# Transformer block in fp32: order of the first loads, engine of two normalized tiles, queue of the last store

## The chip, the core and the metric

The kernel runs on one core of one Trainium2 chip. The metric is device time in microseconds: 620.65 is the median of three runs (619.79 to 624.14). The engines are named as the profile names them: PE is TensorE's matmul and PEld its weight load, DVE is VectorE, ACT ScalarE, POOL GpSimd, SP SyncE. A "q" behind a name (SPq, ACTq) is that engine's instruction queue, from which DMAs are issued.

## What is computed

The input x has 8 batches of 1024 rows with 256 channels, in fp32. Each row is normalized, and the normalized x feeds an attention without softmax and a feed-forward net; both results are added to x.

```python
x = L0_attn_x
xn = _layernorm(x, axis=-1)
x = x + _L0_attn_ref(xn, qkv_w, qkv_b, proj_w, proj_b) + _L0_ffn_ref(xn, W1, b1, W2, b2)

# attention: 16 heads of 16 channels
qkv = (x @ qkv_w + qkv_b).reshape(b, n, 3, H, D)
q, k = _l2norm(q), _l2norm(k)
kv  = einsum('bhnd,bhne->bhde', k, v)
out = einsum('bhnd,bhde->bhne', q, kv)  # then @ proj_w + proj_b

# feed-forward: 256 -> 1024 -> 256
relu(hidden_states @ W1 + b1) @ W2 + b2
```

## The kernel before

**Tiling.** One batch is 1024 rows, held as NT = 8 tiles of 128 rows (one row to a partition), in two halves of HT = 4 tiles. A partition's four rows of a half lie next to each other in memory, so that a load of two tiles reads 2 KB per partition. Most products are made by a scheme with seven block products in place of eight; its sums of blocks are made by POOL and DVE (`sums_of_a`, `sums_of_b`, L179 to L192, L223 to L235).

**Stages of a batch.** Normalize x (`norm_stats`, L239: mean and variance on DVE and the square root on ACT; `norm_scale`, L253: the reciprocal, on DVE; `norm_apply`, L262: xn itself). Turn xn so that channels lie on partitions. Project to q and k (`project`, L311, or `project_by_sums`, L387). Take the norms of q and k. Make the hidden layer (`hidden`, L628). Mix k and xn into a 256 by 256 matrix and fold it with the projection (`mix_g`, `mix_kv`, `mix_m`). Make the second layer together with the attention's product (`second`, L769), add x, and store. The loop over batches is at L935. While one batch is in its hidden and second layers, the next is projected and the one after that is normalized and turned.

**What sets the order.** The kernel is written under a manual schedule (L112): on each engine the instructions run in the order in which the Python code emits them, and every engine's queue is served in that order. DMAs go out on SP's queue, apart from two of the last stores. PSUM is used as banks from a pool of seven (L76, L92), and a new tile of the pool waits until the bank it gets is read out. The x of one batch is in a single buffer (`xs`, one buffer, L99), so the load of the next batch waits until the xn of all eight tiles has been made.

**The start, where two of the three edits are.** SP issues, in this order: tiles 0 and 1 of x (L126), the q and k columns of the weights (L127, L120), tiles 2 to 7 of x in three loads of two tiles (L128, L102), the bias of q and k (L129; `load_qkvb`, L123, spreads 512 numbers over 128 partitions, 256 KB), b1 (L131), w1 in two loads of 512 KB (L134), and the v columns of weights and bias (L135, L136). PE first turns the identity 16 times (L888 to L890). Tiles 0 and 1 are normalized on DVE one by one (L900 to L905), turned by PE and copied out of PSUM by ACT (`turn_tile`, L893 to L898). Tiles 2 and 3 follow as a pair, with xn on ACT (L906 to L908). POOL makes sums of w1 (L909, run at L184).

Then `project(0, ...)` (L931) runs over the eight tiles. For each tile t, PE makes a product of two halves (kc = 0 and 1, L328) and DVE adds the bias while it reads the product out of PSUM (L334). ACT squares the result (L338) and DVE sums the squares (L339); these are held back until tile 3. Between the two halves of tile 1 it emits `tiles_2_3` (L912): turn tiles 2 and 3, then the statistics of 4 and 5 and of 6 and 7, their scales, and their xn. Between the two halves of tile 3 it emits `tiles_4_to_7` (L922): turn tiles 4 to 7, turn b1 (L926), copy it (L927) and make the sums of x on POOL (L928, L929). So DVE's queue around there holds, in order: the bias add of tile 0, the statistics of tiles 4 to 7, their scales, two xn, the bias adds of tiles 1 and 2, the copy of b1, the bias add of tile 3.

The third argument of `norm_scale` says who makes xn:

```python
if on_act:      # one more DVE operation, -mean * rstd ("nmr"), L258
    nc.scalar.activation(xn, xt, AF.Identity, bias=nmr..., scale=rstd...)  # L269
else:
    nc.vector.tensor_scalar(xn, xt, mean, rstd, ALU.subtract, ALU.mult)    # L273
```

For tiles 4 and 5 ACT makes it, for tiles 6 and 7 DVE.

**The end, where the third edit is.** In the last batch the upper half of the result is turned back by PE (`back_on_pe`, L812), added to x by DVE (L822) and stored in three pieces (L867 to L884): tiles 0 and 1 of the half, then tile 2, both issued by ACT, then tile 3, issued by SP. SP issues the four stores of the other half just before (`store`, L808 to L810), and waits for all DMAs at the end.

Of the kernel before, what the change touches and what calls it, by code (L numbers as in the profile page):

```python
# [16 lines left out]
def kernel(  # L17
# [34 lines left out]
    nc = tc.nc  # L52
# [28 lines left out]
    def rows_v(v, b, n):  # L81

        return v[b].rearrange("(n p t) c -> n p t c", n=2, p=P)[n]

    def squares_v(v, b, n, j):


        return v[b].rearrange("(n s r t) (j c) -> n j s r t c", n=2, s=S, r=R, j=R)[n, j]

    def bank(shape, name):  # L90

        return psum.tile(shape, F32, tag="bank", name=name)  # L92
# [3 lines left out]
    def load(b, cuts=(0, HT, NT)):  # L96

        if b not in xs:
            xs[b] = one.tile([P, NT, C], F32, tag="x", name=f"x_{b}")  # L99
        for i, j in zip(cuts, cuts[1:]):  # L100
            n = i // HT
            nc.sync.dma_start(  # L102
                out=xs[b][:, i:j, :], in_=rows_v(x, b, n)[:, i - n * HT : j - n * HT, :]
            )
# [13 lines left out]
    def load_wqkv(cols):  # L118
        for k in range(KC):
            nc.sync.dma_start(out=wqkv_sb[:, k, cols], in_=qkv_w[ts(k, P), cols])  # L120

    def load_qkvb(cols):
        nc.sync.dma_start(out=qkvb_sb[:, cols], in_=qkv_b[cols].partition_broadcast(P))  # L123
# [1 line left out]
    of_qk, of_v = slice(0, 2 * C), slice(2 * C, 3 * C)  # L125
    load(0, (0, 1, 2))  # L126
    load_wqkv(of_qk)  # L127
    load(0, (2, 4, 6, 8))  # L128
    load_qkvb(of_qk)  # L129
    b1_rows = one.tile([FC, P], F32, tag="gT", name="b1_rows")  # L130
    nc.sync.dma_start(out=b1_rows, in_=b1.rearrange("(k p) -> k p", p=P))  # L131
    w1_sb = const.tile([P, KC, INTER], F32, tag="w1", name="w1_sb")
# [120 lines left out]
    def norm_scale(b, tiles, on_act):  # L253
        i, mv, rstd = stats[b, tiles[0]]
        nc.vector.reciprocal(rstd, rstd)
        if on_act:
            nmr = small.tile([P, NT], F32, tag="nmr", name=f"nmr_{b}_{i}")[:, : len(tiles)]
            nc.vector.scalar_tensor_tensor(nmr, mv[:, :, 0], -1.0, rstd, ALU.mult, ALU.mult)  # L258
            for t in tiles:
                stats[b, t] += (nmr,)  # L260
# [500 lines left out]
    def product(dst, lhs, rhs, start, stop):  # L761

        for n, (l, r) in enumerate(zip(lhs, rhs)):
            nc.tensor.matmul(  # L764
                dst, l, r, start=start and n == 0, stop=stop and n == len(lhs) - 1,
                skip_group_check=True,
            )

    def second(b, early=lambda: None, between=lambda: None):  # L769

        xq, hT, hS, qT, (M, Mt) = xqs[b], hTs[b], hSs[b], qTs[b], Ms[b]
        a11, a12, s3, a22 = (
            [hT[:, i + k * FH, ts(n, HP), :, :] for i in range(FH)] + [qT[:, k, ts(n, HP), :, :]]
            for n in range(2) for k in range(2)
        )
        s1, s2, s4 = ([hS[:, s, i] for i in range(FH + 1)] for s in range(3))
        b11, t3, b21, b22 = (
            [w2_sb[:, i + k * FH, ts(m, HC)] for i in range(FH)] + [M[:, k, ts(m, HC)]]
            for k in range(2) for m in range(2)
        )  # L780
        t1, t2, t4 = ([w2t[:, s, i, :] for i in range(FH)] + [Mt[:, s, :]] for s in range(3))

        def tmp(name):
            pool = work if name in ("u2", "yt") else one
            return pool.tile([P, HP, P, 2], F32, tag=name, name=f"{name}_o_{b}")

        def add(dst, p, q):
            nc.vector.tensor_tensor(dst, p, q, ALU.add)
            return dst

        def turn_back(n, m, y):

            yt = tmp("yt").rearrange("p a b c -> p (a b c)").rearrange(
                "p (u w r c) -> p u w r c", w=2, r=R, c=S
            )
            nc.vector.transpose(  # L796
                yt.rearrange("p u w r c -> p u r w c"),
                y.rearrange("p u (s r) w -> p u r w s", r=R),
            )
            xh = xq[:, n, :, :, ts(m, S)].rearrange("p r t c -> p t r c")  # L800
            nc.gpsimd.tensor_tensor(xh, xh, yt.rearrange("p u w r c -> p (u w) r c"), ALU.add)  # L801

        def join(n, m, bank_, u):
            y = tmp("y")
            nc.vector.scalar_tensor_tensor(y, bank_, ob[:, 2, m : m + 1], u, ALU.add, ALU.add)
            turn_back(n, m, y)

        def store(n):  # L808
            for j in range(R):
                nc.sync.dma_start(out=squares_v(out, b, n, j), in_=xq[ts(j, S), n])  # L810

        def back_on_pe(m, y, tiles, name):  # L812


            tp = bank([P, HT, R, S], f"tp{name}_{b}")
            for t in tiles:
                nc.tensor.transpose(
                    tp[:, t].rearrange("p j c -> p (j c)"), y[:, t // 2, :, t % 2], ident
                )
            xh = xs[b].rearrange("p (n t) (j m c) -> n m p t j c", n=2, m=2, c=S)[1, m]  # L820
            at = slice(tiles[0], tiles[-1] + 1)
            nc.vector.tensor_tensor(xh[:, at], xh[:, at], tp[:, at], ALU.add)  # L822

        a, c_, d, e = (bank([P, HP, P, 2], f"po{s}_{b}") for s in "acde")

        if b < B - 1:
            parts = [lambda r: r]
        else:
            parts = [lambda r: r[:, 0], lambda r: r[:, 1, :, 0], lambda r: r[:, 1, :, 1]]
        ds = [parts[0](d)] + [  # L830
            part(bank([P, HP, P, 2], f"po{s}_{b}")) for s, part in zip("fg", parts[1:])
        ]
        product(a, b11, a11, True, False)
        u1 = tmp("u1")
        nc.scalar.copy(u1, a)
        product(c_, t2, s2, True, True)
        u2 = add(tmp("u2"), c_, u1)
        early()
        u3 = tmp("u3")
        for du, part in zip(ds, parts):  # L840
            product(du, t3, [part(r) for r in s3], True, False)
            add(part(u3), du, part(u2))
        between()

        product(e, t1, s1, True, False)
        if b < B - 1:
            join(1, 1, e, u3)
        else:
            y22 = tmp("u1")
            nc.vector.scalar_tensor_tensor(y22, e, ob[:, 2, 1:2], u3, ALU.add, ALU.add)  # L850
        yield
        product(a, b21, a12, False, True)
        y = tmp("y")
        nc.scalar.activation(y, a, AF.Identity, bias=ob[:, 2, 0:1])  # L854
        turn_back(0, 0, y)
        product(e, b22, s4, False, True)
        join(0, 1, e, u2)
        store(0)
        if b < B - 1:
            product(d, t4, a22, False, True)  # L860
            join(1, 0, d, u2)
            store(1)
        else:
            back_on_pe(1, y22, range(HT), "o22")
            y21 = tmp("y")

            def last_store(eng, t, n):  # L867
                eng.dma_start(
                    out=rows_v(out, b, 1)[:, t : t + n, :], in_=xs[b][:, HT + t : HT + t + n, :]
                )  # L870

            for k in range(len(ds) + 1):
                if k < len(ds):
                    part = parts[k]
                    product(ds[k], t4, [part(r) for r in a22], False, True)
                    nc.vector.scalar_tensor_tensor(
                        part(y21), ds[k], ob[:, 2, 0:1], part(u2), ALU.add, ALU.add
                    )
                if k == 1:
                    back_on_pe(0, y21, (0, 1), "o21_0")  # L880
                    last_store(nc.scalar, 0, 2)
                elif k > 1:
                    back_on_pe(0, y21, (k,), f"o21_{k}")
                    last_store(nc.scalar if k == 2 else nc.sync, k, 1)  # L884
        yield


# [24 lines left out]
    def tiles_2_3():  # L912
        for t in (2, 3):
            turn_tile(t)
        norm_stats(0, (4, 5))
        norm_stats(0, (6, 7))
        norm_scale(0, (4, 5), True)
        norm_scale(0, (6, 7), False)
        norm_apply(0, (4, 5))
        norm_apply(0, (6, 7))  # L920

    def tiles_4_to_7():  # L922
# [6 lines left out]
        sums_of_x(0, 1)  # L929

    project(0, {1: tiles_2_3, 3: tiles_4_to_7}, 3, False)  # L931
    s3_of_x(0)
    load(1)
    load_rest()
    for b in range(B):  # L935
# [15 lines left out]
        if b + 1 < B:  # L951
# [4 lines left out]
            def early():  # L956
                if b + 2 < B:
                    norm_stats(b + 2, range(NT))
                    norm_scale(b + 2, range(NT), True)

            def between():
                g_sums(b + 1, 2)
                if b > 0:
                    norms_of_q(b + 1)
# [49 lines left out]
```

## Time and profile before

| what | before |
|---|---|
| median of three runs | 620.65 us (619.79 to 624.14) |
| the profiled execution: its own time | 622.37 us |
| its span | 620.6 us |
| PE busy | 611.1 us, 98% |
| POOL busy | 421.1 us, 68% |
| DVE busy | 411.6 us, 66% |
| ACT busy | 211.8 us, 34% |
| mean granted TensorE clock | 0.995 |
| DMA | 43.32 MB, mean 70 GB/s |

The span runs from the first to the last instruction of the profiled execution; its own time is the device time of that same execution. A line of the timeline shows the start, the length, the engine, the line of code, the operation, what is written and read, and how many instructions were merged. In square brackets stand the idle time before it and what ended it. A line of the chain of waits shows the start, the length and what the chain ran through. A line of the windows shows the stretch, its length, the busy time of PE, PEld, DVE, ACT and POOL, then the granted clock, the DMA engines' busy share and GB/s. A matmul of 128 by 128 with 512 columns in fp32 shows as two records, and some records can be missing.

### The profile page before, as it was taken

To read this page: it belongs to the slowest core of one execution; us is meant where nothing else is said; L and a number is where in the kernel's file an instruction comes from. 1 tells how busy PE (TensorE), PEld (TensorE's weight loads), DVE (VectorE), ACT (ScalarE), POOL (GpSimd) and SP (SyncE) were. 2 spreads that over 40 slices of the span, in tenths; PEclk is the share of its full clock that TensorE was granted. 3 is DMA by queue.
4 is the path that set the end of the run, shared out by engine and by line. 5 is a ranking of instruction groups with operands and counts; after the bars stand their busy time and mean duration, and the time that the engine had idled before them with its cause. 6 is when DMAs were issued, how large, how long until landed. Compare 5 with 4: busy or idle time off the path is not lost.

```text
span 620.6 us, 6646 instructions
## 1 busy us (share of the span) xinstructions
PE 611.1 (98%) x2027; PEld 346.5 (56%) x2027; DVE 411.6 (66%) x736; ACT 211.8 (34%) x361; POOL 421.1 (68%) x346
## 2 busy tenths in 40 slices
PE   8999999999999999999999999999999999999996
PEld 4465446447554566446564474644846557555454
DVE  5778654778647777587756876657865678528823
ACT  4445514252233522344142432415224352103500
POOL 2485997399925998179964799349992499914701
PEclk9899999999999999999999999999999999999999
DMA  6743100590016700285004830058101560004202
GB/s 212 152 69 70 67 1 21 116 191 13 0 45 135 159 2 0 65 156 121 0 1 100 186 54 1 10 127 179 26 0 33 121 118 1 0 5 99 68 1 68
DMA packets 139796, 43.32 MB, mean 70 GB/s; under 512 B 135912, under 2 KB 136816, under 8 KB 139760
## 3 DMA queue, kind: packets, MB, share of 16 engines
q1 hardware_dynamic: 139472, 42.50, 30.7%
q10 hardware_dynamic: 288, 0.39, 0.2%
q8 instruction: 16, 0.26, 0.2%
q14 instruction: 20, 0.16, 0.1%
HBM read 19.80 MB, written 8.39 MB: 45 GB/s over the span
## 4 chain that ended last, share of the span: by engine, by line
PE 95%; DVE 2%; DMA 1%; SPq 0%; issue 0%; ACT 0%; DVEq 0%; ACTq 0%
PE poa L764 11%; PE poe L764 11%; PE pod L764 10%; PE pha L640 8%; PE phe L640 8%; PE phd L640 8%; PE poc L764 6%; PE phc L640 4%; PE pq L328 4%; PE pqe L403 3%; PE pqa L403 3%; PE pqd L403 3%; PE gpe L570 2%; PE gpd L570 2%; PE gpa L570 2%; PE pqc L403 2%
## 5 line engine op out<-in xcount | busy, mean ns | idle before, releaser
L801 POOL TENSOR_TENSOR xq<-xq,yt_o 128x512 f32<-128x512 f32 x30 | 37.9, 1264 | 122.5 <-DVE yt_o L796 122.5
L647 ACT ACTIVATE hT<-hT,b_sb 128x512 f32<-128x512 f32 x96 | 68.9, 722 | 63.2 <-DVE hT L652 58.4
L188 POOL TENSOR_TENSOR hS<-hT 128x512 f32<-128x512 f32 x31 | 46.5, 1500 | 40.2 <-ACT hT L647 40.2
L640 PE MATMUL pha<-xnT,w_sb 128*128 128x512 f32 x128 | 65.4, 592 | 0.0
L764 PE MATMUL poa<-hT,w_sb 128*128 128x512 f32 x128 | 57.6, 592 | 0.0
L381 ACT ACTIVATE sq<-qk 128x512 f32<-128x512 f32 x48 | 28.9, 626 | 71.1 <-DVE qk L409 59.1
L652 DVE TENSOR_TENSOR hT<-phe,u 128x512 f32<-128x512 f32 x64 | 43.7, 684 | 6.7 <-PE phe L640 4.8
L190 POOL TENSOR_TENSOR hS<-hT,hS 128x512 f32<-128x512 f32 x31 | 39.6, 1277 | 2.4
L189 POOL TENSOR_TENSOR hS<-hS,hT 128x512 f32<-128x512 f32 x31 | 39.5, 1274 | 2.4
L796 DVE STREAM_TRANSPOSE yt_o<-y_o 128x512 f32<-128x512 f32 x30 | 33.0, 1100 | 11.4 <-ACT y_o L854 9.1
L192 POOL TENSOR_TENSOR hT<-hT 128x512 f32<-128x512 f32 x31 | 40.0, 1291 | 0.0
L764 PEld LDWEIGHTS poa<-hT,w_sb 128*128 128x128 f32 x128 | 23.8, 190 | 24.7 <-issue 24.2
L640 PEld LDWEIGHTS pha<-xnT,w_sb 128*128 128x128 f32 x128 | 23.8, 190 | 23.4 <-issue 22.5
L666 ACT COPY u<-pha 128x512 f32<-128x512 f32 x32 | 18.4, 575 | 51.6 <-PE pha L640 51.6
L652 DVE TENSOR_TENSOR u<-phc,u 128x512 f32<-128x512 f32 x32 | 21.8, 682 | 19.7 <-ACT u L666 10.6
L647 ACT ACTIVATE hT<-pha,b_sb 128x512 f32<-128x512 f32 x32 | 21.8, 683 | 33.2 <-PE pha L640 33.2
L640 PE MATMUL phe<-xS,w1t 128*128 128x512 f32 x64 | 32.7, 592 | 0.0
L640 PE MATMUL phd<-xnT,w_sb 128*128 128x512 f32 x64 | 32.7, 592 | 0.0
L640 PE MATMUL phc<-xS,w1t 128*128 128x512 f32 x64 | 32.7, 592 | 0.0
L640 PE MATMUL phd<-xnT,w1t 128*128 128x512 f32 x64 | 32.7, 592 | 0.0
L640 PE MATMUL phe<-xS,w_sb 128*128 128x512 f32 x64 | 32.7, 592 | 0.0
L269 ACT ACTIVATE xn<-x,nmr,rstd 128x256 f32<-128x256 f32 x56 | 28.5, 587 | 7.0 <-PE gpd L570 4.1
(200 smaller groups left out, 1318.8 us busy)
## 6 DMA issues: line engine op xcount, KB each, us to landing
xq<-in_L_attn_x_dram SPq DMA_DIRECT2D x60, 128.0 KB, 3.6
out_dram<-xq SPq DMA_DIRECT2D x60, 128.0 KB, 2.9
x<-in_L_attn_x_dram SPq DMA_DIRECT2D x14, 512.0 KB, 4.5
xnT<-turn_x SPq DMA_DIRECT2D x112, 64.0 KB, 2.1
qT<-turn_q SPq DMA_DIRECT2D x112, 64.0 KB, 2.2
w_sb<-in_L_ffn_W_dram SPq DMA_DIRECT2D x2, 512.0 KB, 7.8
w_sb<-in_L_ffn_W_dram SPq DMA_DIRECT2D x8, 128.0 KB, 3.2
x<-in_L_attn_x_dram SPq DMA_DIRECT2D x3, 256.0 KB, 4.3
```

The lines of the kernel that those rows point to most:

```text
L188: eng.tensor_tensor(s1, a21, a22, ALU.add)
L189: eng.tensor_tensor(s2, s1, a11, ALU.subtract)
L190: eng.tensor_tensor(s4, a12, s2, ALU.subtract)
L192: eng.tensor_tensor(a21, a11, a21, ALU.subtract)
L403: nc.tensor.matmul(dst[:, w, :], a[:, g, :, w], rhs, start=start and w == 0, stop=stop, skip_group_check=True,)
L570: nc.tensor.matmul(dst, l[:, t, :], r[:, t, :], start=start and t == 0, stop=stop and t == HT - 1, skip_group_check=True,)
L640: nc.tensor.matmul(dst, lhsT, rhs, start=start, stop=stop, skip_group_check=True)
L647: nc.scalar.activation(block(i, n, m), src, AF.Relu, bias=b1_sb[:, fc : fc + 1])
L652: nc.vector.tensor_tensor(dst, p, q, ALU.add)
L764: nc.tensor.matmul(dst, l, r, start=start and n == 0, stop=stop and n == len(lhs) - 1, skip_group_check=True,)
L796: nc.vector.transpose(yt.rearrange("p u w r c -> p u r w c"), y.rearrange("p u (s r) w -> p u r w s", r=R),)
L801: nc.gpsimd.tensor_tensor(xh, xh, yt.rearrange("p u w r c -> p (u w) r c"), ALU.add)
```

## The change

There are three edits. The bias of q and k is issued after tiles 2 and 3 of x and ahead of tiles 4 to 7. The xn of tiles 6 and 7 of the first batch is made by ACT, with one more small DVE operation for their `nmr`. The last of the three stores of x is issued by ACT instead of SP.

```diff
     load(0, (0, 1, 2))
     load_wqkv(of_qk)
-    load(0, (2, 4, 6, 8))
+    load(0, (2, 4))
     load_qkvb(of_qk)
+    load(0, (4, 6, 8))
     b1_rows = one.tile([FC, P], F32, tag="gT", name="b1_rows")
...
-            def last_store(eng, t, n):
-                eng.dma_start(
+            def last_store(t, n):
+                nc.scalar.dma_start(
                     out=rows_v(out, b, 1)[:, t : t + n, :], in_=xs[b][:, HT + t : HT + t + n, :]
                 )
...
                 if k == 1:
                     back_on_pe(0, y21, (0, 1), "o21_0")
-                    last_store(nc.scalar, 0, 2)
+                    last_store(0, 2)
                 elif k > 1:
                     back_on_pe(0, y21, (k,), f"o21_{k}")
-                    last_store(nc.scalar if k == 2 else nc.sync, k, 1)
+                    last_store(k, 1)
...
         norm_scale(0, (4, 5), True)
-        norm_scale(0, (6, 7), False)
+        norm_scale(0, (6, 7), True)
         norm_apply(0, (4, 5))
         norm_apply(0, (6, 7))
```

## The prediction

> **What bounds it.** I read the page first (its span, granted clock, shares of the chain), then the chain of waits over the first 45 us, then the timeline of each engine around the long link found there, then windows for the clock, and last SP's queue at the end.
>
> ```profile
> span 620.6 us, 6646 instructions
> ...
> PEclk9899999999999999999999999999999999999999
> ...
> PE 95%; DVE 2%; DMA 1%; SPq 0%; issue 0%; ACT 0%; DVEq 0%; ACTq 0%
> ```
>
> TensorE sets the end for 95% of the span, so a microsecond counts only where PE waits, where its clock is low, or after its last matmul. The second digit of the clock row, an 8, is the one dip before the tail. The chain of waits shows what stands ahead of it (start, length, what):
>
> ```profile
> 4.02 6.95 DMA qkvb_sb<-in_L_attn_qkv_b_dram
> ...
> 11.06 0.69 DVE qk L334
> ...
> 14.11 2.32 DVE xn L273 x2
> 16.43 0.61 DVE qk L334
> ...
> 17.34 9.55 PE pq L328 x18
> ```
>
> The bias lands at 10.97; VectorE, whose queue is in order, holds the statistics of tiles 4 to 7 behind the add that needs it (L334), then two xn that take 2.32, then the next add. What PE, ScalarE and GpSimd did meanwhile, from the timelines:
>
> ```profile
> 9.91 3.60 PE L328 MATMUL pq<-wqkv_sb,xnT 128*128 128x512 f32 x8
> 14.42 1.28 PE L897 MATMUL tpx<-ident,xn 128*128 128x128 f32 x6 [0.91 <-ACT xn L269]
> 16.57 0.41 PE L897 MATMUL tpx<-ident,xn 128*128 128x128 f32 x2 [0.87 <-DVE xn L273]
> 17.08 0.26 PE L926 MATMUL b_ps<-ident,b_rows 8*128 8x8 f32 x1
> ...
> 13.78 1.08 ACT L269 ACTIVATE xn<-x,nmr,rstd 128x256 f32<-128x256 f32 x2
> ...
> 14.96 1.32 POOL L184 TENSOR_TENSOR w_sb<-w_sb 128x512 f32<-128x512 f32 x1
> ```
>
> PE ends the first half of tile 3's product at 13.51 and begins its second at 17.27: 3.76 us, of which 0.91 + 0.87 + 0.10 = **1.88 is waiting** and 1.88 (1.28 + 0.41 + 0.19) is transposes. The granted clock follows (window, length, busy of PE, PEld, DVE, ACT, POOL, then PEclk):
>
> ```profile
> 16.50:17.50 1.00, 0.83 (x4) 0.60 (x5) 1.00 (x2) 0.48 (x2) 1.00 (x1) 0.81 0.15 16
> 17.50:18.50 1.00, 1.00 (x2) 0.48 (x3) 0.20 (x2) 0.95 (x2) 1.00 (x2) 0.50 0.86 270
> ...
> 20.50:21.50 1.00, 1.00 (x3) 0.39 (x2) 0.90 (x3) 0.81 (x2) 0.98 (x1) 0.98 1.18 183
> ```
>
> 0.81 means half clock from 17.12, 0.98 full clock from 20.54: 3.42 us at 0.50 with PE busy throughout, so **1.71 us of work lost**.
>
> **The change, part by part.**
>
> (1) Bias ahead of x tiles 4 to 7. No transfer is added; on SP the bias is issued at 3.07 instead of 4.02, the two loads of x 0.48 later each, all behind them at the same place. Landings by the DMA view: x(2,4) issued 2.60 + 4.1 = 6.7; x(4,6) 3.07 + 4.3 = 7.4; x(6,8) 3.54 + 5.3 = 8.8; bias 4.02 + 6.9 = 10.9. So the steps between landings are 0.7, 1.4 and 2.1. If the queue drains in order, the bias follows x(2,4) by 0.7 to 2.1: 7.4 to 8.8, I take 8.0. By one shift of issue alone it would land at 3.07 + 6.9 = 10.0, my outer bound. The x loads follow; the same three transfers still lie ahead of the last landing, so x(6,8) comes by about 10.9; I take 10.5, and x(4,6) 9.3. Outer bound for x(6,8): 4.02 + 8.3, the longest landing of this stretch (w1), 12.3. Its old earliness was worthless: x(6,8) lay unused from 8.8 to 12.55.
>
> VectorE then: nmr of tiles 2 and 3 ends at 8.45 as now; add 0 until 9.15; statistics of tiles 4 and 5 (0.75 + 0.30) from 9.3; of 6 and 7 from 10.5 to 11.55; the reciprocals and two nmr (0.15 each, with ScalarE's 0.29 root of 6 and 7 between) 11.85 for the first nmr, 12.25 for the second. Now the first ends at 13.73. Adds 1 and 2 follow by 13.6, not 17.6.
>
> (2) xn of tiles 6 and 7 by ScalarE. VectorE loses two operations that took 2.32 together; the same form took 0.41 and 0.42 at 4.48 and 5.00, where GpSimd was idle. Here each ended just after one of GpSimd's L184 (13.73 + 1.27 = 15.00, 14.96 + 1.32 = 16.28). I count 2.32, since GpSimd's sums start when w1 lands, which the change doesn't move; if VectorE reached these before 12.38 they would cost 0.83. Added on VectorE: one nmr, 0.16. Added on ScalarE: two ACTIVATE at 0.54 (the pair took 1.08), **ahead of the four copies of tpx**, which now start only after xn of tile 7. ScalarE: xn from 11.95, four by 0.54, done 14.15; copies at 0.41 until 15.8. PE: transposes from 13.51 with xn of 4 and 5 ready (12.5, 13.05), of 6 ready at 13.6 for 14.3, of 7 at 14.15 for 14.7; transposes done by 15.15. The b1 transpose, which now waits for add 1 (0.34 of PEld), finds it done. So tile 3's second half starts at 13.51 + 1.88 = 15.39, and tile 4's product (needed at 16.25) finds its copy made at 14.6. Gain **1.88**. The slack is 0.55: if xn of tile 7 ends after 14.7, each microsecond is lost one for one. SP's load of the next x waits for the last xn (7.3 us of its queue's waits); it leaves at about 14.2 instead of 16.5, with the proj and w2 loads behind it. Its first reader is at 33.77, so this is worth nothing, and costs nothing.
>
> What is late next? GpSimd still ends its sums of x at 21.5; first need is phc, at about 24 after the move, so it hides. VectorE between 16.3 and 25.3 has five adds (0.69) and eight reductions (0.68), 8.9 us in 9, so it just follows; tile 7's product comes at 23.1 and the chain beyond it (adds, roots, L652 up to PE's 0.7 wait at 37.02) moves as a block. Nothing up to the end is tied to an absolute time.
>
> (3) The clock. The Trainium skill (TensorE: Matmul & The Clock Gate, Part 1, "What's actually happening") puts the half clock after at least one idle window of about 3.4 us. Here no wait exceeds 0.91 us and half of the stretch was transposes, yet the clock fell; the row decides: waits summing to half of such a stretch suffice. By the rule this dip isn't due to the waits and stays, gain 0; by the row it goes with them, gain **1.71**. I take the row, for the profiled execution.
>
> (4) The last store, of one tile, by ScalarE. Now it sits on SP behind the four stores of xq:
>
> ```profile
> 614.84 1.36 SPq L810 DMA_DIRECT2D out_dram<-xq  x1
> 616.29 1.04 SPq L868 DMA_DIRECT2D out_dram<-x  x1
> ```
>
> And the windows of that time, which end in DMA share and GB/s:
>
> ```profile
> 616.00:617.00 1.00, 0.00 (x0) 0.00 (x0) 0.00 (x0) 0.00 (x0) 0.00 (x0) 1.00 1.02 288
> 617.00:618.00 1.00, 0.00 (x0) 0.00 (x0) 0.00 (x0) 0.00 (x0) 0.00 (x0) 0.94 1.07 282
> ```
>
> The x it stores is ready at 615.76, and ScalarE's queue has been free since 615.56. From ScalarE it would leave at 615.85 and by the row's 3.4 land at 619.25 instead of 619.7; the xq store of 614.84 lands at 619.34, so 0.35 by this row. But DMA: Bandwidth & Descriptors (Issuing engines are not separate DMA queues) says that issuing from several engines saves only issue time, as all run on the same 16 engines; these are full from 616 to 618 and drain the same bytes, which gives 0. I take **0.2**.
>
> **Sum.** Span 620.6 - 1.88 - 1.71 - 0.2 = 616.8. The profiled execution took 622.37, 1.77 outside the span: 618.6. It lies 1.72 above the median of the runs shown, just what the dip costs, so I read the median as a run without it: 620.65 - 1.88 - 0.2 = 618.6 as well. Predicted 618.6, 0.3% less than now: inside the 1% (6.2 us) that a measurement of this kernel tells from no change.
>
> **Rivals.**
> - The likeliest, chance 0.53: as summed, 618.6; its own range is 617.6 to 619.5 by the 0.55 of slack, the ends of (4) and the scatter of the runs.
> - A part of the wait stays, 0.2: bias at 10.0, or x(6,8) at 12.1. First xn near 13.5, xn of tile 7 done at 15.7, second half of tile 3 at about 16.4: gain 0.9, with 0.2 of the tail 619.6. For it: the bias's 6.9 us to landing; against: three other landings before it came every 0.7 to 1.4.
> - The median run carries the dip too, 0.14: 620.65 - 1.88 - 1.71 - 0.2 = 616.9. For it: the one clock trace there is; against: the 1.72 between it and the median.
> - The gain is given back, 0.06: VectorE or a slow-clock stretch elsewhere takes it, 620.5. Against: the block argument above.
> - Slower, 0.07: **x(6,8) comes too late behind the bias.** From its landing to xn of tile 7 are 3.65 us (10.5 to 14.15); that ended at 16.43 before, so it decides from a landing at 12.8. At 13.8 PE starts 1.0 later than now: 620.65 + 1.0 - 0.2 = 621.5. It needs 9.8 us from issue, more than the 8.3 of the slowest here.
>
> **Chances and range.** 616.7 to 620.4 takes in the first three and half of the fourth's neighbourhood, leaving about 0.15 outside. Over 1% means under 614.4 or over 626.9; no case reaches either, so what I leave there is for a mechanism that I don't see: 0.02 faster, 0.03 slower, 0.95 within.
>
> **What would show it.** Right: the chain's bias link of 6.95 shorter and ending before 9, no VectorE xn from 14 on, ScalarE's four xn in one row from about 12, PE's waits of 0.91 and 0.87 gone, tile 3's second half at about 15.4, PEclk without the 8, last store from ACT near 615.8 less the shift. Wrong: statistics of 6 and 7 waiting on DMA beyond 11, PE waiting on ACT's xn, or a longer tail than 619.7 - 615.76 = 3.9 us from last add to last landing.

## The result, and the profile after

| | before | changed |
|---|---|---|
| median of 22 runs each | 620.67 us | 619.52 us |
| lowest to highest | 619.68 to 624.14 | 618.56 to 621.94 |
| ratio to before, 95% interval | | 0.9977 (0.9966 to 0.9988) |
| profiled execution, its span | 622.37, 620.6 | 619.26, 617.4 |

The change gains about 1.2 us, 0.2%: less than the 1% named ahead, but clear of zero. 618.6 was forecast, and 619.6 for the rival in which a part of the wait stays; the rival's number came out. The two profiled spans differ by 3.2 us, far more than the medians. Why, is the main lesson here.

The page of the changed kernel (lines of its code are one higher than before from L130 on):

```profile
span 617.4 us, 6649 instructions
...
PEclk9999999999999999999999999999999999999999
```

The 8 in the second slice of the clock row is gone. The chain of waits after:

```profile
2.59 4.59 DMA x<-in_L_attn_x_dram
...
8.93 0.61 ACT xn L270
9.58 0.45 PE tpx L898 x2
10.04 0.69 DVE qk L335
...
13.10 0.85 DVE nmr L259
13.97 1.10 ACT xn L270 x2
...
15.71 7.94 PE pq L329 x18
```

The chain now runs through the load of x tiles 2 and 3 (4.59) and names PE's transposes ahead of the add of 10.04. Those write another tile; what the add was waiting for is still the bias, which was issued at 3.06 and landed 6.9 later, at 9.94:

```profile
3.06 0.43 SPq L123 DMA_DIRECT2D qkvb_sb<-in_L_attn_qkv_b_dram x1
...
10.04 0.69 DVE L335 TENSOR_TENSOR qk<-pq,qkvb_sb 128x512 f32<-128x512 f32 x1 [1.14 <-PE tpx L898]
```

The view of the bias's tile gives the two loads that write it (6.9 is this one):

```profile
DMA to landing us min/median/max: 4.9/5.9/6.9
```

The add follows the landing by 0.1, as before (10.96 and 11.06). VectorE's two xn of 2.32 are gone. PE's timeline:

```profile
9.58 0.93 PE L898 MATMUL tpx<-ident,xn 128*128 128x128 f32 x4 [0.72 <-ACT xn L270]
10.35 3.60 PE L329 MATMUL pq<-wqkv_sb,xnT 128*128 128x512 f32 x8
13.79 0.60 PE L898 MATMUL tpx<-ident,xn 128*128 128x128 f32 x4
14.63 0.93 PE L898 MATMUL tpx<-ident,xn 128*128 128x128 f32 x4 [0.23 <-ACT xn L270]
15.49 0.22 PE L927 MATMUL b_ps<-ident,b_rows 8*128 8x8 f32 x1
```

The second half of tile 3's product starts at 15.64 (17.27 before). Of the waits 0.91 + 0.87, 0.23 is left, but one of 0.72 has come up ahead of tile 2: PE ends the first half of tile 3 at 13.95 instead of 13.51. The clock stays at full where it fell before (granted clock is the third number from the end):

```profile
16.00:17.00 1.00, 1.00 (x3) 0.39 (x2) 0.19 (x1) 1.00 (x3) 1.00 (x2) 1.00 0.86 238
17.00:18.00 1.00, 1.00 (x4) 0.49 (x3) 1.00 (x2) 0.20 (x1) 1.00 (x2) 1.00 1.02 377
```

The last add ends 3.23 earlier (612.53 against 615.76): 1.63 from the earlier start, and the other 1.6 I put down to the clock. The tail after it is 4.9 against 4.8.

**Two numbers by which the runs are read.** First, in all twelve profiles without a clock dip after it (the changed kernel and eleven of the experiments), the profiled execution's time less the start of tile 3's second half is 603.57 to 604.00. Apart from the queue of the last store, all that differs between these kernels is ahead of that start. In the two profiles with a dip after it (before and store only) the difference is 605.1 and 605.3, so there the dip cost 1.3 to 1.5. Second, each run has its mean granted clock: 0.997 or more in some, 0.996 or less in others, which are some 2 us longer. These are called runs with a dip. The sorting isn't perfect: the profiled run of bias order only has a dip and a mean of 0.997, and counts as one without. Three later groups of runs of the kernel before hold 56, 57 and 17 of them: with a dip 19, 24 and 9 (40% in all), median 622.3 to 622.5; without, 620.31, 620.55 and 620.64. The changed kernel has 1 of 22 with a dip, and 619.44 without. For the 22 runs of before beside it only times are on record.

### The profile page after: what moved, and what is told of

It is laid out like the page before. It is cut to its first block, busy times and chain, and to the rows that moved or that the text cites. A ratio compares the mean times of both kernels' runs of the same rounds, so it can differ in the third digit from the quotient of the medians.

```text
span 617.4 us, 6649 instructions
## 1 busy us (share of the span) xinstructions
PE 608.3 (99%) x2027; PEld 345.5 (56%) x2027; DVE 409.8 (66%) x735; ACT 212.3 (34%) x363; POOL 420.4 (68%) x346
## 4 chain that ended last, share of the span: by engine, by line
PE 95%; DVE 2%; DMA 1%; ACT 1%; issue 0%; SPq 0%; DVEq 0%; ACTq 0%
PE poa L765 11%; PE poe L765 11%; PE pod L765 10%; PE pha L641 8%; PE phe L641 8%; PE phd L641 8%; PE poc L765 6%; PE phc L641 4%; PE pq L329 4%; PE pqd L404 3%; PE pqa L404 3%; PE pqe L404 3%; PE gpe L571 2%; PE gpd L571 2%; PE gpa L571 2%; PE pqc L404 2%
```

## The experiments

| kernel | tile 3's second half, profile | median of runs without a dip | with a dip | ratio to before (95%) |
|---|---|---|---|---|
| changed | 15.64 | 619.44 | 1 of 22 | 0.9977 (0.9966 to 0.9988) |
| bias order only | 17.66 (dip ahead of it) | 619.63 | 2 of 22 | 0.9982 (0.9971 to 0.9992) |
| ACT's xn only | 16.36 | 620.12 | 5 of 14 | 0.9996 (0.9983 to 1.0010) |
| store only | 16.48 | 620.67 | 8 of 14 | 1.0007 (0.9994 to 1.0019) |
| bias and xn | 15.05 | 619.18 | 1 of 19 | 0.9971 (0.9960 to 0.9982) |
| waits filled | 17.09 | 620.88 | 0 of 22 | 0.9990 (0.9980 to 1.0000) |
| bias not spread | 15.58 | 619.00 | 0 of 10 | 0.9957 (0.9941 to 0.9973) |
| bias in the middle | 16.00 | 620.58 | 7 of 14 | 0.9997 (0.9982 to 1.0013) |
| bias spread by PE | 15.08 | 620.35 | 0 of 22 | 0.9979 (0.9966 to 0.9991) |
| stats first, ACT's xn | 14.54 | 618.16 | 0 of 6 | 0.9946 (0.9931 to 0.9961) |
| stats first | 14.30 | 617.98 | 0 of 6 | 0.9942 (0.9928 to 0.9957) |
| stats first, xn and store by ACT | 13.87 | 618.41 | 0 of 6 | 0.9954 (0.9935 to 0.9972) |
| bias spread by PE, later | 17.82 | 621.81 | 0 of 12 | 1.0002 (0.9989 to 1.0015) |

The first four experiments are compared with the group of 620.31 without a dip, the next four with that of 620.55, the last four with that of 620.64. The ratio is that of all runs, with and without a dip; so a part of it is the dips that a kernel lacks.

**Bias order only.** The kernel before with the first hunk of the change alone.

> Only the bias moves ahead of tiles 4 to 7 of x; xn of tiles 6 and 7 stays on DVE. Theory (each edit takes away a part of PE's wait, the two overlap): the bias lands near 10.0, the statistics of 6 and 7 end near 12.5 as in the changed kernel, DVE begins xn of 6 near 13.1 and is held by GpSimd's running L184 again (two xn take over 2 us), so tile 7 is turned near 15.5 and tile 3's second half begins near 16.1 instead of 17.27: 0.8 to 1.2 us faster. Rival one (the order of loads is all of it): 15.6, 1.2 to 1.6 faster, as the changed kernel. Rival two (order is worth nothing, because the x tiles come as much later as the bias comes earlier): 17.0 or more, within 0.3 of before.

Without a dip it gains 620.31 - 619.63 = 0.7, just below the theory's 0.8 to 1.2. Its profile shows the cost of the move at its worst:

```profile
10.64 1.05 PE L898 MATMUL tpx<-ident,xn 128*128 128x128 f32 x4 [1.84 <-ACT xn L270]
11.49 5.21 PE L329 MATMUL pq<-wqkv_sb,xnT 128*128 128x512 f32 x8
```

x(2,4), with the bias right behind it, landed 5.6 after issue instead of 4.1; PE waited 1.84 for tile 2, and the clock fell behind it (granted 0.83, 0.50 and 0.82 in the windows from 10 to 16); the eight records took 5.21 instead of 3.60. VectorE's two xn took 2.65 beside GpSimd's sums, as the theory had it.

**ACT's xn only.** The last hunk alone.

> Only xn of tiles 6 and 7 goes to ACT; the loads keep their order. Theory: the bias lands near 11.0 as before, ACT's four xn begin at 13.8 and end at 16.0, tile 3's second half begins near 16.7: 0.4 to 0.8 us faster. Rival one (order of loads is all): 17.2, within 0.2. Rival two (the held xn on DVE is all of it): 15.6 to 16.0, 1.2 or more faster. The sum of this run's gain and the bias-only run's gain against the gain of both tells whether they overlap.

0.2 without a dip, below the theory's 0.4 to 0.8, and the interval of its ratio takes in one. In its profile tile 3's second half comes 5.7 after the bias landed, against 6.3 in three profiles with xn on VectorE (see below): 0.6 in the theory's favour, which nine runs don't confirm. 0.7 + 0.2 stands against 1.1 for both (620.31 - 619.18): no overlap is seen, but sums this small don't rule one out.

**Store only.** `last_store(nc.scalar, k, 1)` in the kernel before.

> Only the last store of x is issued by ACT. Theory after the first traces: nothing, since the DMA engines drain the same bytes: last add to end of span stays at 4.84 to 4.87, time within 0.2 of before. Rival (the 0.2 to 0.35 of the prediction): that stretch 4.5 to 4.65, time 0.2 to 0.35 less.

Last add to end of span is 4.9. Over all profiles that stretch is 4.8 to 5.1 in the seven with SP's last store and 4.9 to 5.3 in the seven with ACT's: no gain. PE's timeline shows something else, which matters for the size of the whole change. The start of this kernel is that of before, but here the bias landed at 10.20, not 10.96, and the waits are smaller:

```profile
13.66 1.24 PE L897 MATMUL tpx<-ident,xn 128*128 128x128 f32 x6 [0.36 <-ACT xn L269]
15.77 0.41 PE L897 MATMUL tpx<-ident,xn 128*128 128x128 f32 x2 [0.87 <-DVE xn L273]
```

Tile 3's second half starts at 16.48, 6.3 after the bias, as in the profile of before (10.96 and 17.27).

**Bias and xn, without the store edit.**

> The changed kernel without its store edit. Theory: the same as the changed kernel, 1.1 to 1.6 us faster than before, tile 3's second half at 15.6, last add to end of span 4.84. Rival (the store edit gives 0.2 to 0.35): 0.2 to 0.35 us slower than the changed kernel.

Its median without a dip is 0.26 below the changed kernel's 619.44. With the store-only run (0.36 above before) that hints at a small loss by the store edit; neither is resolved.

**The waits filled.** Transposes of the identity, overwritten by the real ones:

```diff
+        for _ in range(fill):       # 4 for tiles 4 and 7, else 0
+            nc.tensor.transpose(tp[:, 0, :], ident, ident)
         for kc in range(KC):
             nc.tensor.transpose(tp[:, kc, :], xns[0][:, t, ts(kc, P)], ident)
```

> The kernel before, with four transposes of the identity ahead of tile 4's and four ahead of tile 7's (about 0.85 us each time, inside PE's waits of 0.91 and 0.87); their result is overwritten and nothing else changes. Theory (the half clock comes from waits that add up): no dip in the profile near 12 to 20 us, and the upper group of run times (621.6 to 622.6, a third to a half of the runs of before and of the store-only kernel) is gone; the lower group stays at 619.7 to 620.9, median 620.2 to 620.4, ratio about 0.9993. Rival (the dip is not due to the waits): the upper group stays at a third or more of the runs, median as before.

Not one of 22 runs has a dip, against 24 of 57 runs of the kernel before beside it, though PE's path is as late as ever (tile 3's second half at 17.09):

```profile
13.11 0.60 PE L897 MATMUL tpx<-ident 128*128 128x128 f32 x4
14.29 1.26 PE L899 MATMUL tpx<-ident,xn 128*128 128x128 f32 x6 [0.58 <-ACT xn L269]
15.39 0.60 PE L897 MATMUL tpx<-ident 128*128 128x128 f32 x4
16.35 0.44 PE L899 MATMUL tpx<-ident,xn 128*128 128x128 f32 x2 [0.35 <-DVE xn L273]
```

Work that does nothing removed the 2 us of the upper group and cost 0.33 in the others (620.88 against 620.55), which wasn't expected. So the dip comes from the waits.

Why only some runs have it can be read in part from the clock changes in the traces. They come at multiples of 3.41 us after the first one, and the first lies anywhere from 4.4 to 6.9 (12.1 in one kernel, below). The three dips near the start each last 3.41 and begin at the end of such a stretch in which PE idled for 1.73 (before), 1.38 (store only) and 1.90 (bias order only); in all other such stretches up to 30 us it idled for at most 0.99 (with the waits filled), and the clock stayed. So the same waits may fall into one stretch or be shared by two. That this decides about the runs that weren't profiled is argued, not shown.

**Bias not spread.** Leaves out the bias: q and k get numbers of w1 in its place.

```diff
-    load_qkvb(of_qk)
+    nc.sync.dma_start(out=qkvb_sb[:, of_qk], in_=w1[0:P, 0 : 2 * C])
```

> The changed kernel, but in place of the bias spread from 2 KB it loads 256 KB of w1 (2 KB from each of 128 rows) at the same place in the queue; so q and k get other numbers instead of their bias. Theory (128 reads of the same 2 KB are slow in themselves and hold up what is around them): this load lands 4.0 to 5.0 us after issue instead of 5.8 to 6.9, x(2,4) lands 4.0 to 4.4 after issue instead of 4.6 to 5.6. Rival (any 256 KB at this place takes that long, the queue's bytes set it): 5.8 or more, and x(2,4) 4.6 or more.

The load lands 4.8 after issue (5.8 to 6.9 when spread), x(4,6) and x(6,8) behind it 5.0 and 5.2 (6.0 to 7.3), w1 6.3 and 7.1 (6.6 to 8.5). So 128 reads of the same 2 KB are slow and hold what follows (one profile against three). Tile 3's second half gains nothing by it in the profile (15.58): w1 lands early too, GpSimd's sums start at 11.25, and VectorE's two nmr take 1.16 and 1.24 beside them. But x(2,4) lands at 4.6 here too; that half of the theory falls. With another tensor's load between x(2,4) and x(4,6), spread or not, x(2,4) lands later: 4.6 to 5.6 in the four profiles with one, 3.5 to 4.4 in the ten without. Why, stays open.

**Bias in the middle.** `load(0, (2, 4, 6)); load_qkvb(of_qk); load(0, (6, 8))` in the changed kernel.

> The changed kernel with the bias between x(4,6) and x(6,8). Theory (a bias right behind x(2,4) delays it; a bias later comes later itself): x(2,4) lands 3.9 to 4.4 us after issue, the bias near 10.3 to 10.6, tile 3's second half near 15.6 to 15.9, time within 0.3 of the changed kernel. Rival (earliest bias is best): 0.4 or more slower than the changed kernel.

x(2,4) lands 3.8 after issue as the theory had it, but nothing is gained without a dip (620.58 against 620.55), and half of the runs have one. The rival's number came out, but not its reason: the bias landed at 9.45, ahead of the changed kernel's 9.94. PE waits 0.44 and 0.41 for ACT's xn, and ACT for the two nmr, which VectorE makes while GpSimd is in its sums:

```profile
11.67 1.26 POOL L185 TENSOR_TENSOR w1t<-w_sb 128x512 f32<-128x512 f32 x1 [10.37 <-DMA w_sb<-in_L_ffn_W_dram]
12.05 0.90 DVE L259 SCALAR_TENSOR_TENSOR nmr<-mv,rstd 128x2 f32<-128x2 f32 x1
13.02 1.26 POOL L185 TENSOR_TENSOR w1t<-w_sb,w1t 128x512 f32<-128x512 f32 x1
13.06 1.24 DVE L259 SCALAR_TENSOR_TENSOR nmr<-mv,rstd 128x2 f32<-128x2 f32 x1
```

Each ends within 0.02 of the sum beside it (12.95 and 12.94, 14.30 and 14.28); alone an nmr takes 0.16.

**Bias spread by PE.** One row on ACT's queue, then:

```diff
-    WARM = 16
+    WARM = 12
...
+    nc.tensor.matmul(bq_ps, one_row, b_row, start=True, stop=True)
...
+    nc.scalar.copy(qkvb_sb[:, of_qk], bq_ps)
```

> The changed kernel, but the bias of q and k comes as one row of 2 KB on ACT's queue, and PE spreads it over the partitions by a product with a row of ones in place of four of the first 16 transposes; ACT copies it out. Theory (the spread load holds the queue): x(2,4) lands 4.0 to 4.4 after issue, x(6,8) by about 9, the bias is there before 6, PE waits under 0.3 before tile 2 and not at all later, tile 3's second half at 14.9 to 15.3: 0.3 to 0.7 faster than the changed kernel, about 619.0. Rival (the queue's later loads fill the gap, and the start is paced by x(2,4) anyway): within 0.2 of the changed kernel.

The profiled execution, 618.99, was one of the quick ones: PE had no wait from 10.1 on. The runs spread from 617.84 to 621.30 (one at 623.51), with a median that gains 0.2: missed.

**VectorE's order alone, and with ACT's xn.** Loads, queues and sizes as before; only the add of tile 0 goes behind the statistics and scales of tiles 4 to 7 on VectorE:

```diff
                     if kc == 0:
                         within.get(t, lambda: None)()
+                        while held_adds:
+                            held_adds.pop(0)()
...
-                nc.vector.tensor_tensor(qk[:, t, :], pq, qkvb_sb[:, 0 : 2 * C], ALU.add)
+                if within and t == 0:
+                    held_adds.append(add_bias)   # the same tensor_tensor
+                else:
+                    add_bias()
```

> The kernel before with the loads in their old order; on VectorE the add of tile 0 is emitted after the statistics and scales of tiles 4 to 7 instead of ahead of them, and xn of tiles 6 and 7 is made by ACT. Theory (the wait for the bias cost time only because VectorE's queue is in order and held those statistics; and a bias moved right behind x(2,4) pays by delaying x(2,4)): x(2,4) lands 3.8 to 4.4 us after issue, the bias near 11 as before, the statistics of 6 and 7 end by 10.3, ACT's xn of tile 7 by 13.5, tile 3's second half begins at 15.0 to 15.4; runs without a clock dip 1.2 to 1.7 us faster than those of before, and under 1 in 10 with a dip, so 0.3 to 0.7 faster than the changed kernel. Rival (the order of the loads itself matters): at most 0.4 faster than before.

> The same order on VectorE, with xn of 6 and 7 left on VectorE. Theory (those two took 2.32 only because they met GpSimd's sums of w1, which start near 12.4): they come near 11.2, take about 0.8 together, tile 3's second half at 15.0 to 15.6 and the time within 0.3 of the run with ACT's xn. Rival (on VectorE they are slow in themselves, or late behind the add): 2 us for the two, 0.5 or more slower than that run.

Both beat the changed kernel's 619.44 without a dip, and their intervals don't meet its own, though each has only six runs. The bias lands as late as ever (7.3 and 7.0 after issue, near 11), but only the adds wait for it. VectorE and PE with xn left on VectorE:

```profile
10.82 0.16 DVE L255 RECIPROCAL rstd<-rstd 128x2 f32<-128x2 f32 x1
11.01 0.74 DVE L273 TENSOR_SCALAR xn<-x,mv,rstd 128x256 f32<-128x256 f32 x2
11.66 1.88 DVE L338 TENSOR_TENSOR qk<-pq,qkvb_sb 128x512 f32<-128x512 f32 x3
```

```profile
8.97 0.93 PE L906 MATMUL tpx<-ident,xn 128*128 128x128 f32 x4 [0.31 <-ACT xn L269]
9.74 3.61 PE L328 MATMUL pq<-wqkv_sb,xnT 128*128 128x512 f32 x8
13.18 1.04 PE L906 MATMUL tpx<-ident,xn 128*128 128x128 f32 x8
```

The two xn take 0.74, not 2.32, because they come ahead of GpSimd's first sum at 12.31; so once VectorE isn't held, ACT's xn buys nothing (618.16 against 617.98). PE's transposes of tiles 4 to 7 run without a wait, and no run has a dip. The gain without a dip, 2.5 to 2.7, exceeds the 1.2 to 1.7 that was expected: tile 3's second half starts at 14.54 and 14.30, not at 15.0 to 15.4.

**The same with the store by ACT.**

> The stats-first run with ACT's xn, and the last store on ACT as well. Theory (the store edit is worth nothing): within 0.2 of the stats-first run in the runs without a dip. Rival one (it costs, as the store-only run and the changed kernel against its version without it hint): 0.2 to 0.4 slower. Rival two (it gains the 0.2 of the prediction): 0.2 faster.

0.25 above the run beside it, six runs each: the third hint of a small loss, again not resolved.

**Bias spread by PE, later.** The product and the copy are emitted after tile 1's turn.

> The kernel in which PE spreads the bias, with that product emitted after tile 1's turn instead of ahead of tile 0's, so that a late row holds up less. Theory (the spread of 617.8 to 621.3 in the earlier version came from the row's landing, with PE's queue in order behind it): spread under 1.5 us and the median of runs without a dip 0.5 to 1.2 under the earlier version's 620.35. Rival (the spread has another cause): the same spread and median within 0.3.

The theory falls: it is 1.5 slower than the earlier version. Its windows and its product's line show what happened:

```profile
L331 PE MATMUL pq<-wqkv_sb,xnT x8: 592/918/1222, 8.2 to 13.7; 128*128 128x512 f32 x8
```

```profile
8.00:10.00 2.00, 2.00 (x3) 0.84 (x3) 0.33 (x2) 1.27 (x3) 0.00 (x0) 1.00 1.00 397
10.00:12.00 2.00, 2.00 (x4) 0.90 (x3) 0.00 (x0) 0.60 (x2) 1.88 (x2) 1.00 0.63 223
```

From 8.2 to 12.4 a record takes 0.8 to 1.2 instead of 0.592, and the first six fill 4.78 us where the other kernels need 2.85. The granted clock of 1.00 shown for this stretch is no reading: the trace's list of clock changes has its first entry, full clock, at 12.13, and what lies ahead of a first entry is shown as 1.00. In every profile PE is slow ahead of that entry: a transpose takes 0.42 or more there and about 0.3 behind it. In the other thirteen kernels the entry stands at 4.4 to 6.9, so here PE ran at the slow rate for 5 to 8 us more. Ahead of it lie three things that only this kernel has together: twelve warming transposes in place of sixteen, a pause of 0.88 behind them, and the product of the bias, which reads a single row. Which of them counts wasn't tried, nor whether a late entry is also behind the spread of the earlier version, whose profiled run had it at 4.40. The mean clock of a run doesn't show this slow start, since the stretch counts as 1.00.

## Why the prediction was right, and where it was not

- **What bounds it: right.** The time is the start of tile 3's second half plus a constant (603.57 to 604.00), and nothing absorbed the gain on the way: 1.63 at 15.64, 3.23 at the last add.
- **The wait of 1.88: mis-sized.** It was read from one execution in which the bias landed at 10.9 and the start was 17.27. In the three profiles with that order of loads and adds and xn on VectorE, the start is 6.3 after the bias: 10.20 and 16.48 (store only), 10.83 and 17.09 (waits filled), 10.96 and 17.27 (before). The typical run of before without a dip starts at about 620.31 - 603.8 = 16.5 (an estimate from the constant), the changed kernel's at 619.44 - 603.8 = 15.6. So 0.9 to 1.1 is gained without a dip. The step "landings by queue order" put the bias at 8.0; it came at 9.94, my outer bound, with the same 6.9 from issue as before, because the spread load is slow in itself (distinct rows in its place landed at 7.86). The same step left x(2,4) at 6.7 because it is ahead in the queue; it came at 2.59 + 4.6 = 7.2, and PE's new wait of 0.72 is that.
- **VectorE's two xn: right** in the place and the cause, as the line of 0.74 shows; but only because VectorE was late. **The nmr at 0.16: wrong.** The second took 0.84, held by GpSimd's L185 that ran from 12.65 to 13.92, as the xn had been. ACT was busy with xn of 4 and 5 until about 13.9, so it cost 0.1 at most here; with the bias in the middle, where both nmr met a sum, it undid the gain.
- **The clock: the row was right against the rule.** The Trainium skill's one idle window (TensorE: Matmul & The Clock Gate, Part 1, "What's actually happening") would have left the dip where it was and gained 0. The stretches of 3.41 us in the traces agree with its length, but none of the three that dips followed was idle throughout: 1.4 to 1.9 of waiting sufficed. Filling the two waits removed the dip in 22 of 22 runs. The 1.71 that I put on it was 1.3 to 1.6 in the profiled run, by the constant and by the last add. I took the median of before for a run without a dip; it is one, but from the upper end of them (620.65 against 620.31 to 620.64 for their medians), since dips are in 40% of its runs. Taking them away is worth about 0.35 times 2, or 0.7 us, to the mean, and some of it shows in the median too.
- **The last store, 0.2: wrong, 0.** ACT issues it 0.03 after the last add, and it lands 3.8 later instead of 3.4, while SP's last store lands 4.9 instead of 4.5 after its issue. This agrees with the Trainium skill (DMA: Bandwidth & Descriptors, Issuing engines are not separate DMA queues), by which only the time of issuing is saved; the prediction's 0.2 set that against one row of the profile.
- **Of the rivals,** "a part of the wait stays" (chance 0.2) had the bias at 10.0 and the time at 619.6, and both came out; the time by luck. It put tile 3's second half at 16.4, and the profile has it at 15.64, nearer to the main case's 15.39. The profiled run gained 3.1 us of the 3.8 forecast for it; the median gained less because the runs of before start earlier than the one that was read. "Slower" didn't come near: x(6,8) landed at 11.3, not after 12.8. Of the signs of being wrong that were named ahead, PE's waits for ACT's xn came (0.72 and 0.23), and the last landing is 4.0 after the last add, against 3.9.

## What to carry to other kernels

When an in-order engine waits for a late transfer, ask first what stands behind the waiting instruction and whether that can go ahead of it. Here that alone was worth 2.7 us (six runs), while loading the operand earlier was worth 0.7: it still came at 8.9 to 9.9, and x tiles 2 to 7 came later. An operation that looks small can be held by a neighbour: look at what runs beside it. Read a wait from several executions, and set the clock's dips apart by the granted clock of each run, before sizing an edit of one or two microseconds.

## What was not expected of the hardware

- Waits of 1.4 to 1.9 us in all, within 3.41 us of otherwise busy time, halved TensorE's clock for the next 3.41 in three profiles; 40% of the runs of before have the lower mean clock, and useless transposes in the waits prevent it.
- A granted clock of 1.00 at the start of a span says nothing ahead of the first clock change on record (12.13 in one kernel): records of the product took up to 1.2 us there against 0.592.
- A 256 KB load spread from 2 KB landed 5.8 to 7.3 us after issue, where 256 KB of distinct rows took 4.8 at the same place (one profile); and x(2,4) landed about 0.8 later (means of 4.9 and 4.1) when another tensor's load came right behind it.
- An operation of two numbers per partition on VectorE took 0.61 to 1.24 us, instead of 0.16, when it began 0.5 us or more ahead of the end of one of GpSimd's sums of 512 columns: it ended within 0.02 of that sum's end, eleven times in eight profiles.
